# The second transform of the Fourier layer: pairs of channels on four 64x64 tiles of the array in place of fours of channels on the whole array

## The chip, the cores and the metric

The kernel runs as one program on one core of a Trainium2 chip. The metric is the device time of one execution in microseconds (us). Durations of single instructions come from one profiled execution.

## The reference, cut to what matters

The model has four layers. The change lies in the first half of the fourth, which mixes tokens with a Fourier transform; `t` holds 4 images of 4096 tokens with 96 channels, and `w1` widens them to 192.

```python
def _L3_attn_ref(x, w1, bn1_..., r, i, rb, ib, w2, bn2_...):
    h = relu(_bn(einsum('bnc,hc->bnh', x, w1), bn1_...))
    X = fft(h, axis=1, norm='ortho')               # over the 4096 tokens
    rd, idg = diagonal(r), diagonal(i)             # one number per channel
    xr = relu(X.real * rd - X.imag * idg + rb)
    xi = relu(X.imag * rd + X.real * idg + ib)
    y = ifft(xr + 1j * xi, axis=1, norm='ortho').real
    return _bn(einsum('bnh,ch->bnc', y, w2), bn2_...)
...
t = t + _L3_attn_ref(_ln_t(t), ...)
t = t + _L3_ffn_ref(_ln_t(t), ...)
```

## The kernel before

`build` runs the layers one after the other: a state-space layer, a convolution layer, an attention layer, then `fourier` and a quantised feed-forward part (`qffn`). `consts2` loads the weights of the later layers while the convolution runs.

`fourier` (line 1065) writes the transform of 4096 tokens as two matrix products, 128 by 32. The half spectrum needs 65 of the 128 frequencies of the first factor (`K1`). The work is cut into 8 units (4 images, two halves of 96 channels each), and a unit into 4 iterations of 24 channels (`G` = 6 groups of 4 channels), 32 iterations in all. An iteration passes through these steps, each in one engine's order with others between:

- `w1` and `norm` prepare a unit: layer norm of the tokens, the product with `a_w1`, and the Relu that writes `hh`.
- `over_n1` is the first transform: six matmuls with `hh` as weights into the PSUM tile `s_ps`, then the twiddle products `p` on DVE (line 1133) and the sums `f` on POOL (line 1141). The 128 partitions of `f` are 32 positions times 4 channels.
- `over_n2` (line 1143) is the second transform, a 32-point one over those positions. Its weights `bc`, `bs`, `nbs` are 128x128 matrices, the 32x32 transform repeated for each of the four channels (a Kronecker product with a 4x4 identity), so three of four entries are zero. Four matmuls of 390 columns make `xi_ps` and `xr_ps`. DVE then makes `ec` from `xi_ps` (line 1156), ACT makes `av` from `xr_ps` in 12 small pieces (line 1165), and POOL adds and subtracts (lines 1168, 1169).
- `fold` applies the Relu (ACT, line 1175), folds the spectrum to `zz` and `z64` (DVE, lines 1180 and 1183), and copies a negated part (ACT, line 1186).
- `over_k2` is the inverse of the second transform (lines 1198, 1199), copied to `bt` by ACT (line 1200); `row64` does the one remaining frequency of a unit and sends it through DRAM into row 64 of `bt` by two DMAs (lines 1212, 1213).
- `over_k1` is the inverse of the first transform (line 1220, with `gt` loaded from DRAM at line 1217 and copied to `ys` by ACT, line 1222), and `w2` (line 1228) multiplies with `a_w2` and adds to `t` on DVE (lines 1232, 1234).

The order on PE, DVE, ACT and POOL is the one that the program is written in (`manual_schedule`); each of these engines runs its own list from front to back. In iteration j the main steps come as

```python
over_n1(j); fold(j - 2); over_k1(first); over_n2(j - 1); w2(first), over_k1(second); over_k2(j - 3); w2(second)
```

and the `fill` steps (`norm`, `w1` of the next image and `row64`) are dealt out between them. In iterations 0 to 23 there is a fill; iterations 24 to 31 have only `row64`. [...]

Of the kernel before, what the change touches and what calls it, by code (L numbers as in the profile page):

```python
# [9 lines left out]
F32 = mybir.dt.float32  # L10
# [3 lines left out]
AF = mybir.ActivationFunctionType  # L14
# [8 lines left out]
MB = 512  # L23
# [27 lines left out]
class Net:  # L51
# [555 lines left out]
    def consts2(self, wk, small):  # L607
# [78 lines left out]
            nc.vector.tensor_copy(self.a_w2[:, half], ps)  # L686
        self.dft1 = load("dft1", [N1, 2 * 65])
        self.twid = load("twid", [128, 2, 2 * 65])
        self.dft2 = load("dft2", [128, 3 * 128])
        self.dft64 = load("dft64", [128, 2, 128])  # L690


# [372 lines left out]
    def fourier(self, dram, t, h):  # L1065
# [5 lines left out]
        with ExitStack() as ctx:  # L1071
            wk = ctx.enter_context(tc.tile_pool(name="fw", bufs=1))
            pln = ctx.enter_context(tc.tile_pool(name="fp", bufs=1, space=PSUM))
            self.tc.keep_in_program_order(nc.scalar.preload_act_table_set(ACT_EXP_LN))
            nbs, bc, bs = (self.dft2[:, k * 128 : (k + 1) * 128] for k in range(3))
            hh, bt, z64, f, x, av, zz = {}, {}, {}, {}, {}, {}, {}
            ft = [t[:, b * L : (b + 1) * L].rearrange("p (a n) -> p n a", n=N2) for b in range(B)]

# [29 lines left out]
            def w1(b, n):  # L1108

                if n == 0:  # L1110
                    for half in range(2):
                        hh[2 * b + half] = wk.tile([N1, CG, N2, 4], F32, name="hh", tag="hh", bufs=3)
                ps = misc(N1)[:, : 4 * C].rearrange("p (n c) -> p n c", n=2)
                for d in range(2):
                    nc.tensor.matmul(ps[:, d, :], h[:, n + d :: N2], self.a_w1, start=True, stop=True)  # L1115
                for half in range(2):
                    nc.scalar.activation(
                        hh[2 * b + half][:, :, n : n + 2, :].rearrange("p g n c -> p n g c"),
                        ps[:, :, half * C : (half + 1) * C].rearrange("p n (g c) -> p n g c", c=4),
                        AF.Relu,  # L1120
                    )

            def over_n1(i):

                u, g = its[i]
                ps = pln.tile([128, 2, MB], F32, name="s1_ps", tag="s1")
                for d in range(G):
                    a = d % 3 * 2 * K1
                    nc.tensor.matmul(ps[:, d // 3, a : a + 2 * K1], hh[u][:, g + d], self.dft1, start=True, stop=True)  # L1129
                pp = []  # L1130
                for k in range(2):
                    p = wk.tile([128, G, 2, K1], F32, name=f"p{k}", tag=f"p{k}")
                    nc.vector.tensor_mul(  # L1133
                        p.rearrange("p (a g) r k -> p a g (r k)", a=2),
                        ps[:, :, : 6 * K1].rearrange("p a (g k) -> p a g k", g=3),
                        self.twid[:, k : k + 1, None, :].to_broadcast([128, 2, 3, 2 * K1]),
                    )
                    pp.append(p)
                f[i] = wk.tile([128, 2, G, K1], F32, name="f", tag="f", bufs=2)
                for r in range(2):  # L1140
                    nc.gpsimd.tensor_add(f[i][:, r], pp[0][:, :, r, :], pp[1][:, :, 1 - r, :])

            def over_n2(i):

                u, g = its[i]
                cg = units[u][1] * CG + g
                fr, fi = (f[i][:, r].rearrange("p g k -> p (g k)") for r in range(2))
                f.pop(i)
                xr, xi = (pln.tile([128, MB], F32, name=f"x{r}_ps", tag=f"x{r}")[:, : G * K1] for r in "ri")
                nc.tensor.matmul(xi, bc, fi, start=True, stop=False)  # L1150
                nc.tensor.matmul(xi, nbs, fr, start=False, stop=True)  # L1151
                nc.tensor.matmul(xr, bc, fr, start=True, stop=False)  # L1152
                nc.tensor.matmul(xr, bs, fi, start=False, stop=True)
                ec = wk.tile([128, 2, G, K1], F32, name="ec", tag="ec")
                coef = self.v128("id", 0, 96).rearrange("p (k g) -> p k g", k=2)[:, :, cg : cg + G]
                nc.vector.tensor_mul(
                    ec,
                    xi.rearrange("p (o g k) -> p o g k", o=1, g=G).to_broadcast([128, 2, G, K1]),
                    coef[:, :, :, None].to_broadcast([128, 2, G, K1]),
                )  # L1160
                v = av[i] = wk.tile([128, 4, G, K1], F32, name="av", tag="av", bufs=2)
                for d in range(G):
                    at = slice(d * K1, (d + 1) * K1)
                    for k, (w, bias) in enumerate((("rd", "rb"), ("id", "ib"))):
                        nc.scalar.activation(  # L1165
                            v[:, k, d], xr[:, at], AF.Identity, scale=self.v128(w, cg + d), bias=self.v128(bias, cg + d)
                        )
                nc.gpsimd.tensor_add(v[:, 2:4], v[:, 0:2], ec)  # L1168
                nc.gpsimd.tensor_sub(v[:, 0:2], v[:, 0:2], ec)

            def fold(i):

                u, g = its[i]
                v = av.pop(i)
                nc.scalar.activation(v[:, 1:3], v[:, 1:3], AF.Relu)
                z = zz[i] = wk.tile([128, G, 3, K1 - 1], F32, name="zz", tag="zz", bufs=2)
                if g == 0:
                    z64[u] = wk.tile([128, 2, CG], F32, name="z64", tag="z64", bufs=2)
                for k, (one, two, op) in enumerate(((0, 2, ALU.add), (3, 1, ALU.subtract))):
                    nc.vector.scalar_tensor_tensor(  # L1180
                        z[:, :, 1 + k], v[:, one, :, : K1 - 1], 0.0, v[:, two, :, : K1 - 1], ALU.max, op
                    )
                    nc.vector.scalar_tensor_tensor(  # L1183
                        z64[u][:, k, g : g + G], v[:, one, :, K1 - 1], 0.0, v[:, two, :, K1 - 1], ALU.max, op
                    )
                nc.scalar.mul(z[:, :, 0], z[:, :, 2], -1.0)

            def over_k2(i):

                u, g = its[i]  # L1190
                z = zz.pop(i)
                if g == 0:
                    bt[u] = wk.tile([N1, N2, C], F32, name="bt", tag="bt", bufs=2)
                for e in range(0, G, 3):
                    ps = pln.tile([N1, 3, 128], F32, name="i1_ps", tag="i1", bufs=2)
                    for d in range(3):
                        zd = z[:, e + d].rearrange("p k m -> p (k m)")
                        nc.tensor.matmul(ps[:, d], zd[:, 64:], bc, start=True, stop=False)  # L1198
                        nc.tensor.matmul(ps[:, d], zd[:, :128], bs, start=False, stop=True)  # L1199
                    nc.scalar.copy(  # L1200
                        bt[u].rearrange("p n (g c) -> p g n c", c=4)[:, g + e : g + e + 3],
                        ps.rearrange("p g (n c) -> p g n c", c=4),
                    )

            def row64(u):
                ps = misc(CG)[:, :128]
                for k in range(2):
                    nc.tensor.matmul(ps, z64[u][:, k], self.dft64[:, k], start=k == 0, stop=k == 1)
                r = wk.tile([CG, N2, 4], F32, name="r64", tag="r64", bufs=2)
                nc.scalar.copy(r, ps.rearrange("p (n c) -> p n c", c=4))  # L1210
                d = dram.tile([1, N2 * C], F32, name="d64", tag="d64", bufs=2)
                nc.sync.dma_start(d.rearrange("o (n g c) -> g (o n) c", n=N2, c=4), r)
                nc.sync.dma_start(bt[u][64:65].rearrange("p n c -> p (n c)"), d)

            def over_k1(u, n, kept):
# [87 lines left out]
def _constants():  # L1303
# [6 lines left out]
    a, k1 = np.arange(N1), np.arange(65)  # L1310
    th = 2 * np.pi * np.outer(a, k1) / N1
    dft1 = np.concatenate([np.cos(th), -np.sin(th)], 1) / 64
    th = 2 * np.pi * np.outer(np.repeat(np.arange(N2), 4), k1) / L
    tre, tim = np.cos(th), -np.sin(th)
    twid = np.stack([np.concatenate([tre, tre], 1), np.concatenate([tim, -tim], 1)], 1)
    m = np.arange(N2)
    th = 2 * np.pi * np.outer(m, m) / N2
    eye = np.eye(4)
    bc, bs = np.kron(np.cos(th), eye), np.kron(np.sin(th), eye)
    dft2 = np.concatenate([-bs, bc, bs], 1)  # L1320

    th = np.pi * np.outer(2 * m + 1, m) / N2
    dft64 = np.stack([np.kron(np.cos(th), eye), np.kron(-np.sin(th), eye)], 1)
    k1 = np.arange(64)
    tok = 32 * a[None] + m[:, None]
    th = 2 * np.pi * (k1[:, None, None] * tok[None] % L) / L
# [7 lines left out]
        "dft1": dft1.astype(f32),  # L1334
        "twid": twid.astype(f32),
        "dft2": dft2.astype(f32),
        "dft64": dft64.astype(f32),
        "idft": idft.astype(f32),
    }
# [16 lines left out]
def _lay_out(i):  # L1356
# [18 lines left out]
    for k, v in (("c_b1", c["b1"]), ("f2_b1", f["L2_ffn_b1"]), ("f3_b1", f["L3_ffn_b1"])):  # L1375
        v128[k] = v.reshape(3, 128).T
    for k, v in (("rd", np.diagonal(a["r"])), ("id", np.diagonal(a["i"])), ("rb", a["rb"]), ("ib", a["ib"])):
        v128[k] = np.tile(v.reshape(48, 4).T, (32, 1))
    vec128 = np.concatenate([v128[k].reshape(128, w) for k, (_, w) in V128.items()], 1)

    xp = m["xproj_w"]
# [53 lines left out]
```

## Time and profile before

| | us |
|---|---|
| median of 3 runs (4062.0 to 4067.35) | 4064.72 |
| the profiled execution, its own time | 4059.9 |
| its span, first to last instruction | 4058.1 |
| PE busy in the span | 3311.3 |
| the Fourier stage in the trace, 32 iterations | about 3344 to 3919 |

The profiled execution took 1.8 us beside its span, and it lies 4.8 us under the median. In the views, an engine's busy time is the union of its instructions. A matmul of f32 data shows as two records of its line (so four matmuls of `over_n2` are eight records)[...]; the distance from one start to the next is what it costs in a row. The granted clock is the share of full speed at which PE runs; a row of the windows view gives its mean over that stretch.

### The profile page before, as it was taken

The numbers are of one execution on the slowest core, as the hardware profiler recorded it, in microseconds if no ns is written. First come the engines' busy times: TensorE is split into PE (matmuls) and PEld (weight loads), VectorE is DVE, ScalarE is ACT, GpSimd is POOL, SyncE is SP. The second block draws the span as 40 slices with busy tenths as digits, with TensorE's granted clock in tenths as the row PEclk, the third lists the DMA queues.
The fourth block names the chain that finished last, engine by engine and source line by source line (L and its number), as shares of the span: only waits on it lengthen the run. The fifth ranks groups of instructions, "written<-read, shape, count | busy, mean of one in ns | idle before, by whom it ended". The sixth has DMA issues, their size and how long they took to land. (4 is left out here: it accounts for less than half of the span.)

```text
span 4058.1 us, 45524 instructions
## 1 busy us (share of the span) xinstructions
PE 3311.3 (82%) x14174; PEld 1427.9 (35%) x14174; DVE 3193.0 (79%) x2769; ACT 2424.3 (60%) x4647; POOL 2948.0 (73%) x1571
## 2 busy tenths in 40 slices
PE   6888888888888888887788887678999888788977
PEld 3222222222222222222222221277446346555642
DVE  4999999999999999999999999633632673443649
ACT  4666667666667666666766665322445675544557
POOL 2999999999999999999999999511010455333428
PEclk8788878888878888888888887668999998889999
DMA  6567556666757666675675676363000000000111
GB/s 181 136 163 174 136 150 169 159 149 162 175 130 168 168 148 160 160 169 140 159 172 139 160 166 157 94 197 135 0 1 1 1 6 1 29 27 27 45 47 53
DMA packets 183291, 468.13 MB, mean 115 GB/s; under 512 B 53236, under 2 KB 55166, under 8 KB 179968
## 3 DMA queue, kind: packets, MB, share of 16 engines
q1 hardware_dynamic: 183048, 465.21, 45.9%
q8 instruction: 113, 1.85, 0.2%
q14 instruction: 130, 1.06, 0.1%
HBM read 391.53 MB, written 73.50 MB: 115 GB/s over the span
## 5 line engine op out<-in xcount | busy, mean ns | idle before, releaser
L484 POOL TENSOR_TENSOR hs<-hs,crep 128x1024 f32<-128x1024 f32 x768 | 1795.4, 2360 | 27.0 <-DVE hs L478 24.2
L442 PE MATMUL rep<-dbl,sel_b 32*128 32x512 f32 x1152 | 412.2, 793 | 460.2 <-DVE hs L478 433.6
L462 POOL TENSOR_TENSOR up<-udb,brep 128x1024 f32<-128x1024 f32 x256 | 604.0, 2360 | 7.5 <-DMA ud<-du 7.5
L456 ACT ACTIVATE da<-ddb,nega 128x1024 f32<-128x1024 f32 x512 | 585.0, 1150 | 8.5 <-DVE hs L478 6.9
L456 ACT ACTIVATE dap<-ddb,nega 128x1024 f32<-128x1024 f32 x256 | 286.2, 1118 | 419.5 <-DVE hs L478 417.8
L503 PE MATMUL y<-hs,sel_r 128*32 128x512 f32 x3072 | 482.5, 698 | 5.5 <-POOL hs L484 5.5
L478 DVE TENSOR_TENSOR_SCAN hs<-da,state,rep 128x1024 f32<-128x1024 f32 x192 | 450.8, 2348 | 16.7
L478 DVE TENSOR_TENSOR_SCAN hs<-da,state,u 128x1024 f32<-128x1024 f32 x192 | 450.9, 2348 | 10.1
L478 DVE TENSOR_TENSOR_SCAN hs<-dap,state,up 128x1024 f32<-128x1024 f32 x192 | 447.0, 2328 | 6.3 <-ACT dap L456 6.0
L442 PEld LDWEIGHTS rep<-dbl,sel_b 32*128 32x128 f32 x1152 | 110.3, 220 | 762.3 <-issue 511.7
L474 DVE TENSOR_TENSOR u<-udb,rep 128x1024 f32<-128x1024 f32 x256 | 314.7, 1229 | 63.7 <-PE rep L442 41.9
L198 PE MATMUL ps<-n,w_x 97*64 97x512 f32 x1536 | 362.9, 615 | 1.0 <-POOL n L307 1.0
L474 DVE TENSOR_TENSOR rep<-udb,rep 128x1024 f32<-128x1024 f32 x256 | 310.8, 1214 | 0.4
L1020 POOL CAST hq<-y 128x512 fp8e5<-128x512 f16 x192 | 118.4, 641 | 218.2 <-issue 143.0
L1168 POOL TENSOR_TENSOR av<-av,ec 128x780 f32<-128x780 f32 x32 | 58.8, 1837 | 197.5 <-ACT av L1165 197.5
L198 PEld LDWEIGHTS ps<-n,w_x 97*64 97x64 f32 x1536 | 106.8, 139 | 249.9 <-issue 203.5
L503 PEld LDWEIGHTS y<-hs,sel_r 128*32 128x32 f32 x3072 | 66.2, 116 | 359.2 <-issue 192.2
L370 POOL TENSOR_TENSOR du<-delta,xc 128x512 f32<-128x512 f32 x96 | 122.4, 1275 | 70.5 <-ACT delta L354 61.1
L212 PE MATMUL ps<-xc,xproj 64*102 64x512 f32 x384 | 158.3, 986 | 3.5 <-ACT xc L332 3.5
L893 POOL MEMSET h<- 1x4096 f32 x1 | 3.5, 3509 | 212.7 <-DVE n L806 212.7
L346 ACT COPY dbl<-ps 102x512 f32<-102x512 f32 x64 | 34.4, 589 | 205.6 <-PE ps L212 205.6
L478 DVE TENSOR_TENSOR_SCAN hs<-da,rep 128x1024 f32<-128x1024 f32 x64 | 146.5, 2289 | 5.4
(256 smaller groups left out, 6580.8 us busy)
## 6 DMA issues: line engine op xcount, KB each, us to landing
ddb<-dd SPq DMA_DIRECT2D x768, 128.0 KB
udb<-ud SPq DMA_DIRECT2D x768, 128.0 KB
crep<-cd SPq DMA_DIRECT2D x512, 128.0 KB
brep<-cd SPq DMA_DIRECT2D x256, 128.0 KB
dd<-delta SPq DMA_DIRECT2D x64, 384.0 KB
ud<-du SPq DMA_DIRECT2D x192, 128.0 KB
band<-in_band SPq DMA_DIRECT2D x24, 1024.0 KB
gt<-in_idft SPq DMA_DIRECT2D x64, 256.0 KB
```

The lines of the kernel that those rows point to most:

```text
L198: nc.tensor.matmul(ps[rows], w[:, 64 * p : 64 * p + 64], rhs[:, at.start + shift : at.stop + shift], start=k == 0, stop=k == len(ws) - 1, ...
L212: nc.tensor.matmul(ps, w[rows, p], x[rows, p], start=start and p == 0, stop=p == 2)
L370: nc.gpsimd.tensor_mul(u, m["delta"][:, of], m["xc"][:, of])
L442: nc.tensor.matmul(x[:, at], sel_b[rows, order[t][1]], made[k]["dbl"][rows, at], start=True, stop=True)
L456: nc.scalar.activation(da, made[k]["dd", h, j], AF.Exp, scale=nega[:, col : col + 1])
L462: nc.gpsimd.tensor_mul(u, made[k]["ud", h, j], made[k]["brep", g])
L474: nc.vector.tensor_mul(u, made[k]["ud", h, j], x)
L478: nc.vector.tensor_tensor_scan(hs[:, 1:], made[k].pop(("da", t)), u, 0.0 if s == 0 else st, ALU.mult, ALU.add)
L484: nc.gpsimd.tensor_mul(hs[:, :T], hs[:, 1:], made[k]["crep", order[t][1]])
L503: nc.tensor.matmul(made[k]["y", p][row : row + 32], sel_r, made[k]["hs", t][:, at], start=False, stop=True, skip_group_check=True,)
L1020: nc.gpsimd.tensor_copy(q[:, m, :], y2, saturate=False)
L1168: nc.gpsimd.tensor_add(v[:, 2:4], v[:, 0:2], ec)
```

## The change

`over_n2` takes pairs of channels in place of fours. Its weights become the 64x64 Kronecker product with a 2x2 identity, stored twice, on partitions 0 to 63 and 64 to 127. Each of the four old matmuls becomes four, one for each tile of 64 rows (`e`) and 64 columns (`h2`) of the array, with 195 columns each. The two row tiles write into the two banks of one new PSUM tile `x`, which holds the imaginary part at 195 to 389 and the real part at 0 to 194 of each bank. `ec` is made by two DVE instructions in place of one. To make the layout fit, `hh` orders its 128 columns as two pairs of channels, its Relu writes runs of two channels in place of four, `over_k2` copies in four ACT instructions in place of two, and `row64` writes to DRAM with four DMAs in place of one. `over_k2` keeps the whole array, with its own weights `dft2k`. The tables of the constants are permuted to match.

```diff
-        self.dft2 = load("dft2", [128, 3 * 128])
+        self.dft2 = load("dft2", [128, 3 * 64])
+        self.dft2k = load("dft2k", [128, 2 * 128])
...
-            nbs, bc, bs = (self.dft2[:, k * 128 : (k + 1) * 128] for k in range(3))
+            nbs, bc, bs = (self.dft2[:, k * 64 : (k + 1) * 64] for k in range(3))
+
+            lower = [slice(64 * k, 64 * k + 64) for k in range(2)]
...
-                        hh[2 * b + half] = wk.tile([N1, CG, N2, 4], F32, name="hh", tag="hh", bufs=3)
+                        hh[2 * b + half] = wk.tile([N1, CG, 2, N2, 2], F32, name="hh", tag="hh", bufs=3)
...
-                        hh[2 * b + half][:, :, n : n + 2, :].rearrange("p g n c -> p n g c"),
-                        ps[:, :, half * C : (half + 1) * C].rearrange("p n (g c) -> p n g c", c=4),
+                        hh[2 * b + half][:, :, :, n : n + 2, :].rearrange("p g e n c -> p n (g e) c"),
+                        ps[:, :, half * C : (half + 1) * C].rearrange("p n (g c) -> p n g c", c=2),
...
-                fr, fi = (f[i][:, r].rearrange("p g k -> p (g k)") for r in range(2))
-                f.pop(i)
-                xr, xi = (pln.tile([128, MB], F32, name=f"x{r}_ps", tag=f"x{r}")[:, : G * K1] for r in "ri")
-                nc.tensor.matmul(xi, bc, fi, start=True, stop=False)
-                nc.tensor.matmul(xi, nbs, fr, start=False, stop=True)
-                nc.tensor.matmul(xr, bc, fr, start=True, stop=False)
-                nc.tensor.matmul(xr, bs, fi, start=False, stop=True)
+                fi = f.pop(i)
+
+                x = pln.tile([128, 2, MB], F32, name="x_ps", tag="x")
+                for at, first, r, w in ((1, True, 1, bc), (1, False, 0, nbs), (0, True, 0, bc), (0, False, 1, bs)):
+                    for h2, to in enumerate(lower):
+                        for e, rows in enumerate(lower):
+                            nc.tensor.matmul(
+                                x[to, e, at * 3 * K1 : (at + 1) * 3 * K1],
+                                w[rows],
+                                fi[rows, r, 3 * h2 : 3 * h2 + 3].rearrange("p g k -> p (g k)"),
+                                start=first,
+                                stop=not first,
+                                skip_group_check=True,
+                            )
...
-                nc.vector.tensor_mul(
-                    ec,
...
+                for e in range(2):
+                    nc.vector.tensor_mul(
+                        ec[:, :, 3 * e : 3 * e + 3],
+                        x[:, e, 3 * K1 : 6 * K1]
...
                 for d in range(G):
-                    at = slice(d * K1, (d + 1) * K1)
+                    xr = x[:, d // 3, d % 3 * K1 : (d % 3 + 1) * K1]
...
-                    nc.scalar.copy(
-                        bt[u].rearrange("p n (g c) -> p g n c", c=4)[:, g + e : g + e + 3],
-                        ps.rearrange("p g (n c) -> p g n c", c=4),
-                    )
+                    for h2 in range(2):
+                        at = CG // 2 * h2 + g // 2
+                        nc.scalar.copy(
+                            bt[u].rearrange("p n (g e c) -> p e g n c", e=2, c=2)[:, e, at : at + 3],
+                            ps[:, :, h2 * 64 : h2 * 64 + 64].rearrange("p g (n c) -> p g n c", c=2),
+                        )
...
-                nc.sync.dma_start(d.rearrange("o (n g c) -> g (o n) c", n=N2, c=4), r)
+                to = d.rearrange("o (n h g e c) -> h e g (o n) c", n=N2, h=2, e=2, c=2)
+                for h2 in range(2):
+                    for e in range(2):
+                        nc.sync.dma_start(to[h2, e], r[CG // 2 * e : CG // 2 * (e + 1), h2])
                 nc.sync.dma_start(bt[u][64:65].rearrange("p n c -> p (n c)"), d)
```

## The prediction

> **What bounds the kernel now.** I read the page first (PE 82% of the span, but over stages with different limits), then the groups of `over_n2`, the chain of waits inside the Fourier stage, PE's timeline, and the windows view for the granted clock. The groups show what is for sale:
>
> ```profile
> L1150 PE MATMUL xi_ps<-f,dft 128*128 128x390 f32 x64 | 35.6, 647 | 0.0
> L1151 PE MATMUL xi_ps<-f,dft 128*128 128x390 f32 x64 | 34.9, 636 | 0.0
> L1152 PE MATMUL xr_ps<-f,dft 128*128 128x390 f32 x64 | 30.6, 563 | 0.0
> L1153 PE MATMUL xr_ps<-f,dft 128*128 128x390 f32 x64 | 27.3, 508 | 0.0
> ```
>
> These are 128.4 us of PE (32 iterations of four matmuls). Which of them set the end depends on the iteration. In iterations 0 to 23 PE also has the fill. This is the chain in one of them:
>
> ```profile
> 3512.57 1.30 PE xi_ps L1150 x2
> 3513.87 0.81 PE xi_ps L1151 x2
> 3514.68 0.66 PE xr_ps L1152 x2
> 3515.34 0.67 PE xr_ps L1153 x2
> 3516.01 0.02 issue
> 3516.03 0.87 ACT av L1165 x3
> ```
>
> All four matmuls lie on it, and after them either PE itself goes on or, as here, ACT's `av`. Following the chain, I find all sixteen `over_n2` from 3452 to 3754 on it, with 61.6 us. In the last iterations without fill the chain runs round them:
>
> ```profile
> 3787.93 1.33 DVE p L1133 x2
> 3789.26 0.43 issue
> 3789.69 0.55 DVE zz L1180
> 3790.24 0.77 DVE z L1183
> 3791.01 0.48 DVE zz L1180
> 3791.49 0.02 issue
> 3791.51 0.52 ACT zz L1186
> 3792.03 0.48 ACT ys L1222
> ```
>
> and PE, done with `over_n2`, waits for that `ys`:
>
> ```profile
> 3789.86 0.82 PE L1152 MATMUL xr_ps<-f,dft 128*128 128x390 f32 x2
> 3790.51 0.82 PE L1153 MATMUL xr_ps<-f,dft 128*128 128x390 f32 x2
> 3792.55 1.10 PE L1228 MATMUL m_ps<-ys,a_w2s 96*96 96x512 f32 x2 [1.22 <-ACT ys L1222]
> ```
>
> From start to start a matmul costs 0.655 us at full clock, so `over_n2` costs 2.62. Last, the clock. The windows after a gap of 2.37 us before 3510.58 and after one of 1.22 us before 3769.41:
>
> ```profile
> 3510.70:3514.00 3.30, 3.30 (x5) 1.58 (x6) 0.69 (x1) 1.59 (x3) 1.26 (x1) 0.50 0.26 72
> 3769.40:3772.80 3.40, 3.40 (x25) 2.87 (x26) 1.93 (x2) 3.40 (x13) 0.00 (x0) 1.00 0.08 23
> ```
>
> The third number from the right is the clock: half after the long gap, full after the short one.
>
> [...] twelve records of 64 rows and 512 columns (L212) take 3.69 us at 1000.05, in pairs that start 5 ns apart, and eight records of 128*32 (L503) take 1.07 us at 1003.67, where one such record alone streams for 0.43. [...]`row64`: its first record starts 0.205 us after the last of L1129 in place of 0.11, and the next full-array one as late again, so 0.09 a side. No 64x64 tile is in the trace. [...] the trace's half stretches are 3.41 or 6.83 us long. [...] in the convolution DVE starts on the first quarter of `cv_ps` at 2702.74, only after the tile's last matmul, started at 2702.36, though its own quarter was made some 2.8 us earlier.
>
> **The change part by part.**
>
> *The matmuls.* 16 matmuls are 32 records in 8 rounds of four tiles. A record of 195 columns is half of 390, whose records start 0.328 apart: 0.165. Eight rounds are 1.34, and entering and leaving the mode 0.19: 1.53 in place of 2.62, so **1.09 us less** per iteration. Loading 64 columns took 0.139 us (L198), and loads of different tiles start 7 ns apart, so they hide under a 0.165 round. From above, the price is 2.83 if only two tiles run together[...].
>
> *Banks.* `xi` and `xr` had a bank each, and `ec` (DVE) and `av` (ACT) ran side by side: 3792.30 and 3792.41. Now both readers share both banks, so `av` should wait for `ec`'s half of its bank (half of 0.97 is about 0.5 us), and `ec` for the `xr` matmuls. Where the chain leaves through `av`, the gain falls to about 0.54. Bounds: 0 if reads needn't wait, 1.05 if `av` waits for both halves. Behind the waiting `av` on ACT stand `ys` and the `bt` copies, with 0.6 us or more to spare in the iterations I followed; POOL's sums wait for it too.
>
> *Iterations 8 to 23.* Of the sixteen, twelve leave through PE (12 x 1.09 = 13.1) and four through `av` (4 x 0.54 = 2.2): **15.2 us less**. Part of them ran at half clock; but the half windows hang on the gap before, and what follows then runs in them instead, so I count full-clock time only.
>
> *Iterations 1 to 7.* No chain reaches so far back. Of the first three, one feeds `av` directly and two wait for `fold` or `norm`; I take 3 of 7 at 1 us: **3 less** (0 to 7).
>
> *Iterations 24 to 31.* PE's earlier end buys nothing: the chain is DVE, ACT. It costs: the gap of 1.22 grows by 1.09 to 2.3. Of the nine PE gaps of 2.1 to 2.6 us in this stage eight had half clock at their end or within 1.8 us; none of 1.0 to 1.3 us before 3870 set it off. [...] Half a window lost is 1.7 us, all of it on the chain (`w2` to `over_n1`, 6.7 us long), and 3.2 where two windows follow (one in eight). Seven gaps x (0.55 x 1.7 + 0.12 x 3.2) = **9.2 more** (0 to 22). The second loop, `fold`, `ec`, `av`, POOL, Relu, has 0.5 us to spare in its 11.58 and loses it to `av`'s wait: 0.5 more (0 to 4).
>
> *row64.* Three more DMA issues of 0.33 on SP, and 8-byte runs, twice as many. Before, 3.87 us went from the write's issue to the read's. Only the last unit's is on the chain (PE waits 2.53 for it at 3891.23): **1.7 more** (1 to 4). The others have 4 us or more to spare; `gt`, queued behind on SP, also has.
>
> *The rest.* The four `bt` copies: a 384-element copy takes 0.48, two of 192 about 0.32 each as the Relu of `hh` shows (0.35), so 0.3 more ACT per iteration, in front of ACT's wait for POOL; without that cover, 8 us over 24 iterations. The runs of two channels in `hh`: same element count, 0 (to 1). One more constant load of 0.3 to 0.45 us issue on SP ahead of the `band` loads: 0.4 (0 to 1). Two half `ec` add 0.1 of DVE, free while DVE waits for PE.
>
> **Sum** against 4059.9: -15.2 - 3 + 9.2 + 0.5 + 1.7 + 0.4 = -6.4, so 4053.5. The profiled execution was 4.8 under the median; on the median's scale **4058.3**, say 4058. What a measurement here can tell from no change is 0.2%, 8.1 us.
>
> **The rivals.** (a) *The clock holds* in the last iterations[...]: without the 9.2 it is -15.6, 4049. For it: one gap of 2.14 us passed without loss. Against: eight of nine didn't. (b) *The tiles don't run four at a time*, so the change doesn't do what it says. With pairs only `over_n2` costs 2.83: 16 x 0.21 = 3.4 more, 2 for `av`'s wait, 2.6 for the small parts, about 4073. One after another, 32 x 0.165 = 5.3, it is 2.85 more in 19 chain iterations and 1.6 more in the seven late ones, about 4134. It turns at a round of 0.30 us in place of 0.165. Against it: L212 and L503 run side by side; for it: no row-and-column tile has been seen. (c) *Clock and banks both at their bounds*: two windows lost each time (22.4) and `av` held by both halves (6 more in all): +12.8, 4077.
>
> **How the numbers follow.** The forecast 0.50, the clock holding 0.28, the tiles 0.12, the bounds 0.10. The forecast itself spreads 7 us either way, so about 0.09 of its half falls beyond -8.1 and a little beyond +8.1; (b) and (c) mostly end slower. That gives faster 0.36, same 0.43, slower 0.21. The range 4043 to 4075 leaves out the serial tiles and a gain with no loss at all; the likeliest case alone is 4051 to 4066.
>
> **What would show it.** Right: 32 records per `over_n2` starting in fours within 30 ns, about 1.5 us from first to next instruction; PE's gap before L1228 near 2.3 us in the last iterations and half clock after most of them; `av` starting after the first half of `ec`; the wait at the last `row64` near 4 us. Wrong: starts of records 0.165 apart, `over_n2` as long as before, or a period of the filled iterations (20.4 us) that doesn't fall by about 1.

## The result and the profile after

The kernel after takes 4066.23 us (median of 12 runs, 4058.39 to 4075.37), the kernel before 4066.74 us beside it (12 runs, 4062.0 to 4074.02). The ratio is **1.0002, 95% interval 0.9994 to 1.001**: no change that can be measured. A ratio is taken over the runs and can differ a little from the quotient of the medians; one execution of e7b, 5104.04 us at a mean clock of 0.545, is left out of its ratio. The profiled execution of after took 4070.7 us of its own time, that of before 4059.9; the medians say that most of these 10.8 us are the two executions and not the kernels. So I read stretches and periods in the traces, and leave sums to the medians.

The groups by line show that the tiles do what they were meant to do. A group's columns are engine, operation, output and input with their shape, the count, then busy time and mean ns of one, then idle time ahead of it and what ended it:

```profile
L1157 PE MATMUL x_ps<-f,dft 64*64 64x195 f32 x1024 | 68.1, 420 | 2.3 <-issue 2.3
L1179 ACT ACTIVATE av<-x_ps,vec 128x65 f32<-128x65 f32 x384 | 117.2, 429 | 52.3 <-DVE ec L1168 36.8 <-PE m_ps L1118 15.0
```

and the second of them in the kernel before:

```profile
L1165 ACT ACTIVATE av<-xr_ps,vec 128x65 f32<-128x65 f32 x384 | 117.0, 424 | 48.4 <-PE xr_ps L1153 48.4
```

The 1024 records are busy for 68.1 us, where the four lines of before had 128.4. In the trace the starts come in fours, 7 ns apart, and a new four about every 0.165 us. The lines of `av` show the new wait: ACT stood idle ahead of `av`, and 36.8 us of that ended with DVE's `ec`, where before all of it ended with PE's `xr_ps`. The chain of waits in a filled iteration of after, and then in one of its last iterations:

```profile
3525.63 1.20 PE m_ps L1118 x4
3526.83 1.48 PE x_ps L1157 x32
3528.31 1.13 PE m_ps L1118 x4
```

```profile
3796.68 0.47 DVE zz L1194
3797.15 0.91 DVE z L1197
3798.06 0.95 DVE ec L1168 x2
3799.01 0.02 issue
3799.03 0.02 ACTq L1179
3799.05 0.05 issue
3799.10 1.16 ACT av L1179 x4
```

In the first, `over_n2` costs 1.48 us between two other PE instructions; before, it was 2.62 at full clock. The second is new: before, the chain went from `zz` by ACT to `ys`; now it goes on through `ec` and `av`, and PE gets its second `ys` only after all twelve `av`. The timeline has the same place with the idle time ahead of an instruction in brackets:

```profile
3795.03 1.55 PE L1157 MATMUL x_ps<-f,dft 64*64 64x195 f32 x32
3797.98 1.02 DVE L1168 TENSOR_TENSOR ec<-x_ps,vec 128x390 f32<-128x390 f32 x2
3798.23 1.10 PE L1253 MATMUL m_ps<-ys,a_w2s 96*96 96x512 f32 x2 [1.65 <-ACT ys L1247]
3799.10 3.67 ACT L1179 ACTIVATE av<-x_ps,vec 128x65 f32<-128x65 f32 x12 [0.92 <-DVE ec L1168]
```

`av` starts after **both** halves of `ec` (1.02 and an idle ACT for 0.92), not after the first. PE's gap ahead of `w2` is 1.5 to 2.7 us in these iterations. The windows view with the clock third from the right, the last iterations of before and then of after, from the start of iteration 23 to that of iteration 31:

```profile
3744.50:3844.30 99.80, 88.41 (x538) 67.50 (x537) 61.81 (x72) 56.19 (x154) 47.12 (x32) 1.00 0.15 44
```

```profile
3732.90:3841.80 108.90, 87.09 (x730) 71.10 (x729) 62.28 (x80) 57.72 (x170) 47.85 (x33) 0.94 0.18 40
```

The clock falls from 1.00 to 0.94, and the stretch grows by 9.1 us. Last, PE around the last `row64`, before and then after:

```profile
3893.76 1.99 PE L1220 MATMUL m_ps<-gt,bt 128*96 128x128 f32 x8 [2.54 <-issue]
```

```profile
3890.38 1.10 PE L1253 MATMUL m_ps<-ys,a_w2s 96*96 96x512 f32 x2 [0.72 <-ACT ys L1247]
3899.46 1.99 PE L1245 MATMUL m_ps<-gt,bt 128*96 128x128 f32 x8 [7.98 <-issue]
3902.18 2.02 PE L1253 MATMUL m_ps<-ys,a_w2s 96*96 96x512 f32 x2 [0.72 <-ACT ys L1247]
```

The wait is 7.98 us in place of 2.54, and in both what follows starts at half clock (1.99 for eight records, in place of 1.04).

The traces by stretch, in us, with the half-clock time in parentheses. All are one profiled execution each; the experiments are told below.

| kernel | iterations 0-7 | 8-22 | 23-30 | 31 and tail | shortest late period |
|---|---|---|---|---|---|
| before | 98.3 (24) | 301.8 (65) | 99.8 (0) | 75.0 (10) | 11.57 |
| after | 98.8 (28) | 292.6 (74) | 108.9 (14) | 85.2 (27) | 12.17 |
| e1 | 99.1 (28) | 298.4 (75) | 109.3 (17) | 71.9 (7) | 12.17 |
| e2 | 102.5 (31) | 319.5 (99) | 111.4 (20) | 82.8 (20) | 12.4 |
| e3 | 102.1 (24) | 311.6 (68) | 107.0 (3) | 77.8 (14) | 12.17 |
| e4 | 99.2 (31) | 289.5 (58) | 108.1 (10) | 81.9 (14) | 12.17 |
| e5b | 97.2 (20) | 287.9 (65) | 106.3 (14) | 85.7 (27) | 11.64 |
| e6b | 96.7 (24) | 288.4 (72) | 105.0 (14) | 82.9 (24) | 11.57 |
| e7b | 98.6 (20) | 297.3 (44) | 101.4 (3) | 69.8 (3) | 11.58 |
| e8b | 96.7 (20) | 290.7 (68) | 110.2 (24) | 72.7 (10) | 11.65 |
| e9 | 97.2 (22) | 291.6 (70) | 102.4 (7) | 72.4 (7) | 11.64 |
| e10 | 95.5 (20) | 294.7 (82) | 109.1 (20) | 66.7 (3) | 11.94 |
| e11 | 96.6 (21) | 298.7 (48) | 101.6 (0) | 64.7 (0) | 11.79 |

A stretch begins with the first matmul of its first iteration's `over_n1`; the tail ends with the first matmul of `qffn`. An iteration's period goes from its `over_n1` to the next; of the eight periods of 23 to 30 the first still has a fill (18.8 to 22.4 us).

So in these two executions iterations 8 to 22 took 9.2 us less, and about that much came back in the last iterations and again in the tail. The theory to test: three things give the gain back, (1) `ec` and `av` now share a PSUM tile, (2) the clock drops more often because PE idles longer, (3) `row64`'s four DMAs are late for the last unit. The rivals: that the small tiles cost something themselves, and that one of the three does all of it.

### The profile page after: what moved, and what is told of

Read it like the earlier page. It is cut to its first block, busy times and chain, and to the rows that moved or that the text cites. A ratio compares the mean times of both kernels' runs of the same rounds, so it can differ in the third digit from the quotient of the medians.

```text
span 4068.9 us, 47235 instructions
## 1 busy us (share of the span) xinstructions
PE 3295.8 (81%) x14942; PEld 1430.0 (35%) x14942; DVE 3196.2 (79%) x2801; ACT 2427.4 (60%) x4711; POOL 2947.7 (72%) x1571
## 5 line engine op out<-in xcount | busy, mean ns | idle before, releaser
L478 DVE TENSOR_TENSOR_SCAN hs<-da,state,rep 128x1024 f32<-128x1024 f32 x192 | 450.9, 2348 | 16.7
L1182 POOL TENSOR_TENSOR av<-av,ec 128x780 f32<-128x780 f32 x32 | 58.8, 1837 | 202.7 <-ACT av L1179 202.7
```

Source lines behind the costliest of these rows:

```text
L478: nc.vector.tensor_tensor_scan(hs[:, 1:], made[k].pop(("da", t)), u, 0.0 if s == 0 else st, ALU.mult, ALU.add)
```

## The experiments

Each ratio is against the kernel before on the same chip. Its median differed from chip to chip (4064.13 beside e1 to e4, 4067.15 beside e5b to e8b, 4058.82 beside e9 to e11), so times are compared within one of these three sets, and ratios across them.

### e1: after, row64's first half one iteration sooner

```diff
-                nc.sync.dma_start(bt[u][64:65].rearrange("p n c -> p (n c)"), d)
+                d64[u] = d
+            def row64_in(u):
+                nc.sync.dma_start(bt[u][64:65].rearrange("p n c -> p (n c)"), d64.pop(u))
...
+                    if (j - 6) % PER == 0 and 0 <= (j - 6) // PER < len(units):
+                        fill.append(lambda j=j: row64((j - 6) // PER))
...
-                        fill.append(lambda j=j: row64((j - 7) // PER))
+                        fill.append(lambda j=j: row64_in((j - 7) // PER))
```

> The kernel after, with row64 cut in two: its matmul, copy and four DMA writes come one iteration sooner, the read into row 64 of bt stays where it was. Stretches of the Fourier stage so far, from the start of over_n1 8, 23 and 31 to the first matmul of qffn: middle 301.8 us before, 292.6 after; last iterations 99.8 and 108.9; tail 75.0 and 85.2. Theory A (the four small-run writes are slow, PE waits 7.98 us for the last of them, and the half clock that follows is their doing too): the wait vanishes, the tail falls to about 72, the whole kernel is 10 to 14 us faster than the kernel after, so about 0.3% faster than before. Rival R1 (the tail is long because PE came into it with the clock down): the wait goes but the tail keeps over 80 us, and the gain is under 6 us.

Measured: 4061.53 us (13 runs), ratio 0.9997 [0.9988, 1.0006]. The tail went from 85.2 to 71.9 us, 13.3 less. The DMA issues in the timeline, after and then e1:

```profile
3888.07 1.73 SPq L1237 DMA_DIRECT2D d<-r  x4
3889.90 0.36 SPq L1242 DMA_DIRECT2D gt<-in_idft  x1
3897.15 0.23 SPq L1238 DMA_DIRECT2D bt<-d  x1
```

```profile
3880.91 1.73 SPq L1237 DMA_DIRECT2D d<-r  x4
3888.74 0.23 SPq L1241 DMA_DIRECT2D bt<-d  x1
```

In after, the read back is issued 9.08 us after the writes began (3.87 before), and only then can PE go on. In e1 the writes start 8.6 us sooner, counted from the start of iteration 31, and PE no longer waits for the read. The wait and the tail went as theory A said; its 10 to 14 us for the whole kernel did not come. The ratios (1.0002 for after, 0.9997 here) are 2 us apart, with intervals that overlap, and in this execution iterations 8 to 22 took 5.8 us more than in after. Cause 3 holds for the tail, and alone it gives no verdict against before.

### e2: after, ec and av by halves in turn

```diff
                 for e in range(2):
                     nc.vector.tensor_mul(ec[:, :, 3 * e : 3 * e + 3], ...)
-                for d in range(G):
-                    xr = x[:, d // 3, ...]
+                    for d in range(3 * e, 3 * e + 3):
+                        xr = x[:, e, ...]
```

> The kernel after, with the instructions of ec and av written bank by bank: half of ec, six av, the other half of ec, six av, so that the first av waits for one half of ec only. Theory A (av waits for both halves of ec because the banks are shared, which made the last iterations' period 12.18 us where the clock held, against 11.58 before): av starts about 0.5 us sooner after ec's start, the period falls to 11.6 to 11.8 where the clock holds, 3 to 5 us less in all. Rival R2 (the last iterations lose by the half clock alone): no change of the period beyond that of the clock, total within 2 us of the kernel after.

Measured: **4097.28 us**, ratio 1.0087 [1.0073, 1.0102]. The forecast, 3 to 5 us less than after, was wrong. I had meant to let `av` start after its own bank's `ec`. It did, and a new wait came in its place:

```profile
3799.85 0.55 DVE L1169 TENSOR_TENSOR ec<-x_ps,vec 128x390 f32<-128x390 f32 x1
3800.44 1.89 ACT L1179 ACTIVATE av<-x_ps,vec 128x65 f32<-128x65 f32 x6 [0.39 <-DVE ec L1169]
3802.36 0.56 DVE L1169 TENSOR_TENSOR ec<-x_ps,vec 128x390 f32<-128x390 f32 x1 [1.96 <-ACT av L1179]
3802.96 1.89 ACT L1179 ACTIVATE av<-x_ps,vec 128x65 f32<-128x65 f32 x6 [0.63 <-DVE ec L1169]
```

The second `ec` waits 1.96 us for six `av` that read the *other* bank. So the program's waits between DVE and ACT go by PSUM tile, not by bank: whoever comes second in the written order waits for all that came first on that tile. Over the stage DVE waited 64.9 us for it. This explains why `av` waits for both halves in after.

### e3: before, with the shared tile alone

The whole array, four channels, all layouts as before; only `xr_ps` and `xi_ps` become one tile of two banks, as in after, with eight matmuls of 195 columns and two `ec`.

```diff
-                xr, xi = (pln.tile([128, MB], F32, name=f"x{r}_ps", tag=f"x{r}")[:, : G * K1] for r in "ri")
+                x = pln.tile([128, 2, MB], F32, name="x_ps", tag="x")
+                for at, first, r, w in ((1, True, 1, bc), (1, False, 0, nbs), (0, True, 0, bc), (0, False, 1, bs)):
+                    for e in range(2):
+                        nc.tensor.matmul(x[:, e, at * 3 * K1 : (at + 1) * 3 * K1], w, ...)
```

> The kernel before, whole-array matmuls kept, but each of the four cut into two of 195 columns that write into the two banks of one tile, as in the kernel after, with ec in two halves and av reading the same banks. Theory A: the sharing of banks alone makes the last iterations' period 12.2 us in place of 11.58 (99.8 us become about 104) with the clock at full speed, and costs the middle 0 to 5 us; in all 4 to 9 us slower than before. Rival R2: the period stays 11.6 and the time is that of before within 2 us.

Measured: **4081.72 us**, ratio 1.0046 [1.0033, 1.0058], 17.6 us more than before and well above the forecast of 4 to 9. The eight matmuls are not what costs: they take 2.65 us at full clock, the four of before 2.62. The late periods go from 11.58 to 12.18 us, the same as in after, at a nearly full clock (0.98 for the stretch). The chain has after's shape:

```profile
3785.59 0.95 DVE ec L1162 x2
...
3786.63 1.16 ACT av L1173 x4
3787.79 0.01 issue
3787.80 2.49 ACT av L1173 x8
3790.29 0.44 ACT ys L1230
```

Sharing the tile is thus the whole of the 0.6 us by which the late period grew, and it can cost more than the forecast's 2.7 us for the stage. From e3 to after, the tiles and the new layout save 19.0 us in iterations 8 to 22 and 3.3 in the first eight; that is the gain that was looked for.

### e4: after, the late matmuls twice

The sixteen matmuls are issued twice from iteration 23 on, with the same result; PE then has 1.3 us more to do where it otherwise waits.

```diff
-... (0, False, 1, bs)):
+... (0, False, 1, bs)) * (2 if i >= 23 else 1):
```

> The kernel after, with the sixteen tile matmuls of over_n2 done twice over from the 24th iteration's on (the first pass's sums are overwritten), so that PE is busy there as long as in the kernel before. Theory C (my prediction: a longer PE gap in the last iterations lowers the clock): PE's gap before w2 goes back to 1.2 us or less, no half-clock window in the last iterations, 108.9 us become 103 to 105, what stays over 99.8 being the period of 12.18. Rival (the period of 12.18 is all there is): no change, or slower by the added matmuls.

Measured: 4064.29 us, ratio 1.0002 [0.9993, 1.0012]. PE's gap ahead of `w2` is 1.05 us in place of 2.37, as expected, but the last iterations take 108.1 us, not the 103 to 105 of the forecast. The seven late periods are 12.18, 12.54, 12.18, 12.19, 12.28, 12.18, 12.17, where after had 13.22, 13.56 and 13.22 among four of 12.17 or 12.18: three long ones are gone, 3.0 us in sum. So in this execution of after the clock took only some 3.5 us of the last iterations (1.04 + 1.38 + 1.04 over 12.18), and sharing took 7 x 0.6 = 4.2. The first period, the one with a fill, was 2.2 us longer than in after, and no gain is left in the median.

### e5b: after, with two PSUM tiles

The two banks as two tiles; nothing else.

```diff
-                x = pln.tile([128, 2, MB], F32, name="x_ps", tag="x")
+                x = [pln.tile([128, MB], F32, name=f"x{e}_ps", tag=f"x{e}") for e in range(2)]
```

> The kernel after, with x as two PSUM tiles of one bank each in place of one tile of two banks; instructions, order and addresses stay. Theory A (e2 and e3: the program's waits go by PSUM tile, and ec and av reading the same tile one after the other cost the 19 us that the matmuls save): av's first six pieces now wait for the first ec half alone, so av starts about 0.5 us sooner. The period of the last iterations falls from 12.18 to about 11.7, the middle (iterations 8 to 23) by 4 to 8 us, in all 6 to 12 us less than after: 4055 to 4060. Rival B (the waits go by bank in any case, or the time lies in the two tables of matmuls and not in av's wait): no difference from after within 0.1%, period 12.18. Rival C (av's second half now waits for the second ec, which runs behind other DVE work): gain of 1 to 3 us only.

Measured: **4056.25 us**, ratio 0.9972 [0.996, 0.9983]. Theory A holds: four of the seven late periods are 11.64 or 11.65 (the other three, with half clock, 13.21 to 13.60), and the lines of `ec` and `av` in a late iteration are:

```profile
3801.39 1.02 DVE L1168 TENSOR_TENSOR ec<-x_ps,vec 128x390 f32<-128x390 f32 x2
3801.98 3.66 ACT L1179 ACTIVATE av<-x_ps,vec 128x65 f32<-128x65 f32 x12 [0.39 <-DVE ec L1168]
```

ACT now waits 0.39 us in place of 0.92, for the first half alone. By the ratios, on two chips, this one line is worth 0.30% of 4066, 12 us; by the sums of the four stretches it is 8.4 us. The same edit on top of e1 (e8b against e1) gives the same two figures. So I count it as 8 to 12 us. In the late iterations it is the 0.5 us that the forecast had taken for the change itself.

### e6b: after, no PSUM shared between DVE and ACT

`ec` is made from `f` in SBUF.

```diff
-                        x[:, e, 3 * K1 : 6 * K1]
-                        .rearrange("p (o g k) -> p o g k", o=1, g=3)
-                        .to_broadcast([128, 2, 3, K1]),
+                        fi[:, 1:2, 3 * e : 3 * e + 3].to_broadcast([128, 2, 3, K1]),
```

> The kernel after, where ec multiplies the imaginary part of the first transform (SBUF tile f) in place of the second's (PSUM tile x): the Fourier product is changed in this one operand, all instructions, sizes and the four-tile matmuls stay, and DVE no longer reads the banks that ACT reads. Theory A (the tiles' gain is there and is eaten by ec and av sharing the banks): av starts right behind the matmuls, the middle falls from 292.6 to about 283, the last iterations from 108.9 to about 98 to 101 (period 11.6 or less), in all 14 to 22 us less than after, 4044 to 4052. Rival B (the new layout itself, small ACT pieces and the mode changes, takes it): 0 to 6 us less. Rival C (the clock takes it: PE idles more and drops to half speed more often): the middle falls, and the half-clock time of the Fourier stage grows by 15 us or more, 5 to 10 us less in all.

Measured: 4057.88 us, ratio 0.9978 [0.9966, 0.9991]. No theory has it whole. `av` starts right behind PE, and the shortest period is before's 11.57, as A had it; but the total is that of e5b, not the 4044 to 4052 of A. What is missing lies in three late periods of 13.2 us, with half clock (14 us of it in the last iterations), and in iterations 8 to 22, 5.4 us above the forecast with 72 us of half clock. Once `av` needn't wait for both halves, what is left of sharing is 0.07 us a late period. That the clock takes the rest is likely and not shown by this run.

### e7b: before, with the early row64

The edit of e1, on the kernel before.

> The kernel before, with row64's matmul, copy and write to DRAM one iteration sooner and its read at the old place (the same edit that took 13.3 us from the tail of after). Theory A (before waits 2.54 us for that read at the last row64, and no half clock follows from it): tail 75.0 to about 72.5, in all 1 to 4 us less, within 0.1% of before. Rival B (the wait in before also costs a half-clock window): tail 65 to 70, 5 to 10 us less.

Measured: **4053.93 us**, ratio 0.997 [0.9959, 0.9981], 13.2 us less than before. A (1 to 4 us) is wrong. The tail is 69.8 us, as in rival B: 5.2 less, 2.5 of the wait and the rest of half clock, which in before follows that wait (3893.76, eight records in 1.99 us) and is gone here. That explains 5 of the 13; iterations 8 to 22 had 20 us less half clock in this execution, and whether the edit causes that isn't shown. In e11, which has the same edit, the gain was 6.5 us on another chip.

### e8b: after, two tiles and the early row64

> The kernel after, with both edits: x as two PSUM tiles of one bank, and row64's first half one iteration sooner. Theory A (the two are independent): the gains of the two add up, tail about 72, last iterations with a period of about 11.7, 4050 to 4056, 10 to 16 us less than after and faster than before by 0.2 to 0.35%. Rival B (half-clock windows move about and take one of them): no more than the better of the two alone, 4057 to 4061.

Measured: 4054.29 us, ratio 0.9966 [0.9952, 0.9979]. Inside A's range, 2 us better than e5b, and **no better than e7b** on the same chip: with these two faults mended, the change is still worth nothing that can be measured. By stretch against e7b: 1.9 less in iterations 0 to 7, 6.6 less in 8 to 22, 8.8 more in 23 to 30, 2.9 more in the tail. Five of the seven late periods are 13.15 to 13.58 in place of 11.65. PE in two of these iterations:

```profile
3791.63 2.02 PE L1256 MATMUL m_ps<-ys,a_w2s 96*96 96x512 f32 x2 [2.37 <-ACT ys L1250]
3797.70 1.02 PE L1256 MATMUL m_ps<-ys,a_w2s 96*96 96x512 f32 x2
3804.78 1.74 PE L1256 MATMUL m_ps<-ys,a_w2s 96*96 96x512 f32 x2 [2.37 <-ACT ys L1250]
```

After a gap of 2.37 us two records take 2.02 or 1.74 us, where they take 1.02 to 1.10 at full clock. The gap is before's 1.22 and the 1.1 us that the tiles saved.

### e9: e8b, with the late matmuls twice

The edits of e5b, e1 and e4 together.

> The kernel after with two PSUM tiles and the early row64 (as e8), and in the last iterations (from 23) the sixteen matmuls of the second transform are issued twice, the second pass writing the same values again: about 1.5 us more PE work in the place where PE else waits for ys. Theory A (in e8 what is left of the tiles' gain is lost to the clock: five of seven periods at 13.2 in place of 11.65, because PE's gap ahead of w2 is 2.3 us long): all periods 11.6 to 11.7, half clock of the last iterations from 23.9 to under 4 us, last iterations 110.2 to about 99 to 102, in all 6 to 10 us less than e8: 4044 to 4048. Rival B (the longer periods come from something else that the tiles moved, and the clock follows them): periods stay above 12.5 and the time within 3 us of e8 or above it.

Measured: **4046.74 us**, ratio 0.9971 [0.996, 0.9983]; the lowest time of all, on a chip where before took 4058.82. In the trace A holds for the periods: all late periods but one are 11.64 to 11.66 (one 12.01), and the stretch of the last iterations, e8b and then e9, is

```profile
3726.50:3836.70 110.20, 90.64 (x730) 73.92 (x729) 62.11 (x80) 58.10 (x170) 46.59 (x31) 0.89 0.15 36
```

```profile
3728.40:3830.80 102.40, 92.03 (x954) 76.25 (x953) 62.43 (x80) 57.11 (x170) 46.64 (x31) 0.97 0.16 39
```

224 more records, the clock at 0.97 in place of 0.89, and 7.8 us less. PE's gap is now 1.05 us:

```profile
3802.05 1.10 PE L1256 MATMUL m_ps<-ys,a_w2s 96*96 96x512 f32 x2 [1.05 <-ACT ys L1250]
```

That the same work issued twice shortens this stretch, in e4 and again here, points to the clock as the cause of the long periods. The late periods of all traces agree: in the five kernels whose usual gap there is 2.37 us (after, e1, e5b, e6b, e8b) 17 of 35 are 1 us or more above the shortest, in the five where it is 1.05 to 1.23 (before, e3, e4, e7b, e9) none of 35. In the ratios e9 and e8b can't be told apart (0.9971 and 0.9966 on two chips), so how much of the 7.8 us reaches the median is open. On its own chip e9 is the fastest version, 12 us under before and 5.6 under e11; against e7b and e8b, on another chip, it has no lead that can be seen.

### e10 and e11: the first over_k1 ahead of fold

In iterations 24 and later, on e8b (e10) and on e7b (e11):

```diff
+                    early = blocks and j >= len(its) - 8
+                    if early:
+                        main.append(lambda: over_k1(*blocks[0], kept))
                     if 2 <= j < len(its) + 2:
                         main.append(lambda j=j: fold(j - 2))
-                    if blocks:
+                    if blocks and not early:
```

> The kernel after with two PSUM tiles and the early row64 (as e8), and in iterations 24 to 31 the first over_k1 is placed ahead of fold, so that ACT makes ys before it copies the negated part of zz. Theory A (in the last iterations PE's gap ahead of w2 is the wait for ys, which stands behind p, three DVE instructions of fold and ACT's copy; that gap is what sets half clock): the gap shrinks to under 1 us, no half clock in the last iterations, the period falls to about 10 to 10.6, last iterations 84 to 92, in all 18 to 25 us less than e8: 4029 to 4036. Rival B (another wait of the same loop takes its place, over_k2 waiting for zz, at nearly the same time): period 11 to 11.6, 5 to 12 us less than e8.

> The kernel before with the early row64 (as e7) and in iterations 24 to 31 the first over_k1 ahead of fold, as in e10. It asks whether the tiles are worth anything once the last iterations don't wait for ys. Theory A (the tiles take 6 to 12 us from iterations 8 to 23, and 1.09 from each late iteration where PE is then the bound): period 11 to 11.6, this kernel 10 to 18 us slower than e10. Rival B (the tiles' gain in the middle is lost again somewhere else, as e7 against e8 has it): within 4 us of e10.

Measured: e10 4053.95 us (21 runs), ratio 0.9984 [0.9977, 0.9992]; e11 4052.33 us (21 runs), ratio 0.998 [0.9973, 0.9987]. Both theories of e10 missed: the periods are 11.94 to 13.39, longer than in e8b at full clock. The gap moved to the second `w2` and the chain runs round ACT:

```profile
3798.20 3.07 ACT av L1179 x10
3801.27 0.44 ACT ys L1250
3801.71 0.04 issue
3801.75 1.10 PE m_ps L1256 x2
3802.85 1.97 PE s_ps L1133 x12
```

From there it goes on through the next iteration's first `over_k1`, its `ys`, the Relu, `fold` and `ec` back to `av`: the second `ys` stands behind twelve `av`, and the first now stands ahead of the Relu that these `av` wait for in the end. What e10 and e11 still tell: with the same order, the full array has late periods of 11.79 to 11.94 and no half clock in the last iterations, and the tiles 11.94 to 13.39 with 20 us of it. e11's rival B held.

## Why the prediction was right, and where it was not

The class and the time were right (4058 with 4043 to 4075, measured 4066.23; "same" the likeliest). Several terms of the sum were not, and they offset each other: that the number came so close was in part luck.

*The matmuls* (1.53 in place of 2.62): right. 1.48 to 1.55 in the trace, fours 7 ns apart, 0.165 us a round. No trace of before had shown 64x64 tiles; that they run four at a time was an estimate, and these starts show it: rival (b) is out.

*Iterations 8 to 23* (15.2 less): right in PE's work. If I count half-clock time at half its length, iterations 8 to 22 go from 269.5 us to 255.3 in after, 14.2 less; but after has 10 us more half clock there, so half of that, 5 us, is given back and 9.2 is left.

Over more kernels it is 269.5, 275.1 and 274.9 us in the three full-array kernels with their own PSUM tiles (before, e7b, e11; mean 273.2), and 252.6 to 261.0 in the eight tiled kernels other than e2 (mean 256.5), 16.7 less; the stretches themselves differ by 7.6, since half clock is 52 us in the mean of the three and 70 in that of the eight. Whether the tiles cause these 18 us isn't shown. They are single executions; before has 65 us, and the eight range from 58 to 82. PE's idle time (the stretch less PE busy) is about the same with the tiles (57.9 to 58.8 us in the three, 56.5 to 61.9 in the eight). The mean granted clock of the whole span, over the runs in the ratios, is lower with tiles in the pairs on one chip (0.8575 in e7b and 0.8510 in e8b; 0.8589 in e11, 0.8544 in e9 and 0.8519 in e10), but it doesn't say in which iterations: e4, which differs from after (0.8518) from iteration 23 on alone, has 0.8556, as before beside it (0.8559). So the forecast's "I count full-clock time only" left out something that these traces show, and its cause is open.

*Iterations 1 to 7* (3 less): nothing in after (98.8, before 98.3). Where `av` isn't held up it is 95.5 to 97.2, but e11, with the whole array, has 96.6, so a gain isn't shown.

*Banks*: the mis-sized step is "about 0.5 us" taken from bounds of 0 and 1.05. The upper one is what happened: `av` waits for both halves. I had read in the trace that waits go by tile (DVE on `cv_ps` starting at 2702.74, after the last matmul, started at 2702.36), priced that for PE and DVE, and then assumed banks for DVE and ACT. In the last iterations it made 0.6 us a period, 4.2 in all (forecast 0.5); e5b shows 8 to 12 us for it over the whole kernel, where the forecast had 2.7. That `av` would have to wait for the half of `ec` on its own bank was an estimate, and it was not shown: in none of the runs here do `ec` and `av` read one bank at the same time. What decided was how the program's waits are drawn around a tile (e2: 1.96 us of waiting for `av` on the other bank).

*The clock in iterations 24 to 31* (9.2 more): that half clock goes with the longer gap is shown by e4 and e9 (gap 1.05 us in place of 2.37; half clock in these iterations 10 us in e4 and 14 in after, 7 in e9 and 24 in e8b), the size depends on the version. The forecast's shares, 0.55 and 0.12 of the gaps, were an estimate; 17 of the 35 late periods with a usual gap of 2.37 us came out long. In after it was 3.5 us over three long periods; with two tiles, where the gap is the forecast's own 2.3 (measured 2.37), e8b's five long periods sum to 8.2 us above 11.65.

The traces show more closely when the clock changes. In the Fourier stage of all 13 the clock changes only on a grid of 3.41 us. Of the full-clock windows of that grid with less than 1.2 us of PE idle time (no PE instruction in the views), half clock came next after 4 of 1234; with more than 2.0 us, after all of 196; between, after 99 of 310. And of the half-clock windows with more than 0.3 us of idle time only 2 of 126 were followed by full clock, of those with less than 0.1 us 282 of 288. So a gap of 2.37 us brought half clock where more than 2.0 us of it lay within one window, and could pass where the grid cut it: in after, the gap that ends at 3759.28 has 2.16 us in one window, and the clock is 0.50 from 3760.53 to 3763.94; the one that ends at 3786.05 is cut into 0.74 and 1.63, and the clock stays full. That this is why the long periods come and go is an inference from these counts. Not every half stretch is one or two windows, as the forecast has it: one in before is 17.07 us, five windows.

*row64* (1.7 more): wrong in size. The wait grew by 5.44 us (7.98 against 2.54), above the range's 4, and 17 us more half clock followed it. Three more issues were priced at 0.33 each, 1.0 in all, and took 1.40; the smaller runs were left nearly free. I can't divide the other 3.8 us between the runs of 8 bytes and the four separate DMAs; that wasn't tried.

*The constants, the `bt` copies, `hh`* (0.4 in all): nothing larger shows. ACT is busy for 117.2 us with `av` as before, and for 33.9 with the `bt` copies in place of 30.9, 0.1 us an iteration; the copies were never on the chain that I followed.

So the sum of terms was -6.4, and the measured difference -0.5 in medians: PE's work fell about as forecast. In after, the clock of the last iterations gave back less than its 9.2; sharing, `row64` with the half clock behind it, and the half clock in iterations 8 to 22 gave back more than the forecast had for them. Of rival (c), clock and banks both at their bounds, the half on the banks is what happened.

## What to carry to other kernels

Before counting a cheaper instruction as a gain, ask what its engine does in the time set free: on a PE that was already waiting 1.22 us, five of seven late periods in e8b came to 13.15 us or more where the others took 11.65, for 1.1 us of matmuls saved in each, and the same matmuls issued twice took less time there (102.4 us in e9, 110.2 in e8b). When two engines read one PSUM tile, give each bank a tile of its own: one line of allocation was worth 8 to 12 us here, about what the cheaper matmuls took out of iterations 8 to 22 (9.2). And give a round trip through DRAM an iteration of slack before making its writes smaller: in after PE waited 7.98 us for one, and the iteration of slack in e1 took 13.3 us off the tail.

## What I had not expected of the hardware

A round trip of 12 KB through DRAM took 2.87 to 4.53 us from the first issue to the read's when written in one DMA with runs of 16 bytes (eight in before), and 7.18 to 9.88 when written in four with runs of 8 (eight in after). And PE lost its full clock for 3.41 us after a gap of 2.37 us (0.50 from 3760.53 in after), though it is busy for 80% of the last iterations of after (87.09 of 108.9 us). In these traces the change went with the idle time within one window of a grid of 3.41 us: more than 2.0 us of it were followed by half clock in 196 of 196 full-clock windows, and of the half-clock windows with more than 0.3 us of it only 2 of 126 were followed by full clock.
